# Fetching one chunk of edges in 68 with row DMAs of SyncE instead of a gather of GpSimd, in a four-layer graph network

## The chip, the cores and the metric

The kernel runs on one core of a Trainium2 chip. The metric is the device time of one execution in microseconds, from the first to the last instruction of the core with what lies around it; the time before is the median of three runs.

## The reference, cut to what matters

A graph of 12,500 nodes and 212,500 edges, sorted by destination, with 128 features per node. Four layers follow each other, each `x = x + layer(relu(layernorm(x)))`:

```
gat_conv twice:   e = leaky_relu(alpha_src[src] + alpha_dst[dst]); softmax of e over each dst
                  out = segment_sum(alpha[:, None] * h[src], dst)
transformer_conv: alpha = sum(q[dst] * k[src]) per head; softmax over each dst
                  agg = segment_sum(a * v[src], dst); then wo, layer norm, feed forward, layer norm
max layer:        msgs = z[dst] @ Wd + z[src] @ Ws + edge_weight * ww + bm
                  agg = segment_max(msgs, dst); then two dense layers
mean layer:       segment_sum(x[src], dst) / max(count, 1)
```

Each of the five aggregations (gat twice, transformer, max, mean) reads a row of a node table for every edge: `h[src]`, `k[src]` and `v[src]`, and so on.

## The kernel before

The kernel first prepares the edge lists: `prepared` (L406) brings the source numbers of the edges into the tile `IDX` (L463), in which column k holds the 128 source numbers of chunk k, one per partition. After that come five *edge passes*, `edge_pass` (L1298), one for each aggregation: gat1, gat2, attn, max and sum. Between them the dense work of a layer is done tile by tile at the end of each node tile (`after_gat1` and the like).

A pass walks over 98 node tiles of 128 nodes (T = 98). The 1,661 chunks of 128 edges are dealt out in *units* of 17 chunks (U = 17), a unit to a node tile, with a margin of three chunks to both sides. A unit's chunks form six groups (GS = 3), the last of them with two chunks. For every chunk `gather` (L1207) issues one indirect DMA from GpSimd's queue: 128 rows of the pass's table, picked by a column of `IDX`, into a slot of the tile `g` (L1212). The tables are rows of 66, 130, 264, 128 and 129 floats in the five passes, and `g` has 18, 18, 17, 20 and 24 buffers of one group each. `e1`, `chain` and `e2` work on the edges of a group; `batch` (L1240) multiplies one-hot matrices with the edge rows into `acc`; `ends` (L1271) loads `gt`, takes the result out of `acc`, merges it with `gt` (`listed_too`, L1280), and does the layer's dense work.

The order of the work is written out by hand. `edge_pass` puts each step as a Python generator at a *round*, with a rank; a unit is 24 rounds long (RU = 24), a group has 4. In every round the live generators advance by one step, the lowest rank first, and this fixes the order of instructions on each engine's queue. The gather of group i of unit u stands at round 24(u - 1) + 4i, its first use (`e1`) 24 rounds later. The loads of `se`, `st`, `x` and `gt`, and the stores of results (`o`, `xx`, `kv`, `u` and so on), all stand on SyncE's queue (SP), at their rounds, and SP issues them in this order: it waits at a store until the result is there, and what is behind it waits too. SP's DMAs use eight semaphores in turn, so that each DMA waits until the one eight before it has landed.

Of the kernel before, what the change touches and what calls it, by code (L numbers as in the profile page):

```python
# [65 lines left out]
def gnn_kernel(ctx, tc, a, out):  # L66
# [17 lines left out]
    ww_d = dram.tile([3, D], BF16, name="ww_d")  # L84
    feat_d = dram.tile([T, 5, EW], BF16, name="feat_d")
    last_d = dram.tile([T, 5, EW], BF16, name="last_d")
    ewf_d = dram.tile([3, CP * P], BF16, name="ewf_d")
    first_d = dram.tile([1, (CP + 16) * P], BF16, name="first_d")
    xd = dram.tile([NP, D], F32, name="xd")
# [198 lines left out]
    def chunks(out, x, on):  # L288

        o = out.rearrange("p (r b) -> p r b", b=RC)  # L290
        for b0 in range(0, RC, 4):
            n = min(4, RC - b0)
            px = psum([P, 4, P], "b", "px")
            for b in range(n):
                PE.transpose(px[:, b, :], x[:, (b0 + b) * P:(b0 + b + 1) * P], ident)
            yield
            on(o[:, :, b0:b0 + n].rearrange("p r b -> p b r"), px[:, :n, :])
# [108 lines left out]
    def prepared(wp):  # L406
        tn_i = wp.tile([P, 1], I32, name="tn_i")
        GP.iota(tn_i, pattern=[[0, 1]], base=0, channel_multiplier=P)
        tid = wp.tile([T, 1], I32, name="tid")
        GP.iota(tid, pattern=[[0, 1]], base=0, channel_multiplier=1)  # L410
        tn = wp.tile([P, 1], F32, name="tn")
        V.tensor_copy(tn, tn_i)
        tn1 = wp.tile([P, 1], F32, name="tn1")
        V.tensor_scalar_mul(tn1, tn, -1.0)
        tn2 = wp.tile([P, 1], F32, name="tn2")
        V.tensor_scalar_add(tn2, tn, float(P))
        yield

        w = rd_[:, 1:EW + 1]
        eq = wp.tile([T, EW - P], BF16, name="eq")
        long_ = wp.tile([T, 1], F32, name="long_")
        V.scalar_tensor_tensor(eq, w[:, P:], 0.0, w[:, :EW - P], op0=ALU.add, op1=ALU.is_equal,
                               accum_out=long_)
        yield
        f = wp.tile([T, 2], F32, name="f")
        V.tensor_scalar(f[:, 0:1], rd_[:, 0:1], tn[:T, :], long_, op0=ALU.is_ge, op1=ALU.max)
        V.tensor_scalar(f[:, 1:2], rd_[:, EW + 1:], tn2[:T, :], f[:, 0:1], op0=ALU.is_lt,  # L430
                        op1=ALU.max)
        V.tensor_scalar_min(f[:, 1:2], f[:, 1:2], 1.0)
        yield
        p2 = psum([P, P], "mm", "p2")
        PE.transpose(p2[:1, :T], f[:, 1:2], ident[:T, :T])
        yield
        flag = wp.tile([1, T], F32, name="flag")
        V.tensor_copy(flag, p2[:1, :T])
        zr = wp.tile([1, T], F32, name="zr")
        V.memset(zr, 0.0)  # L440
        ord_ = wp.tile([1, T], F32, name="ord_")
        V.tensor_tensor_scan(ord_, flag, zr, 0.0, op0=ALU.add, op1=ALU.add)
        V.tensor_copy(NOV, ord_[:, T - 1:T])

        at = wp.tile([1, T], F32, name="at")
        V.scalar_tensor_tensor(at, flag, -float(2 * T), ord_, op0=ALU.mult, op1=ALU.add)
        V.tensor_scalar_add(at, at, float(2 * T - 1))
        yield
        pfl = psum([P, P], "mm", "pfl")
        PE.matmul(pfl[:, :T], ones[0:1, :], flag, start=True, stop=True)  # L450
        p3 = psum([P, P], "mm", "p3")
        PE.transpose(p3[:T, 0:1], at, ident[0:1, 0:1])
        yield
        V.tensor_copy(FLAG, pfl[:, :T])
        at_i = wp.tile([T, 1], I32, name="at_i")
        V.tensor_copy(at_i, p3[:T, 0:1])
        GP.indirect_dma_start(out=list_d, in_=tid, in_offset=None,
                              out_offset=bass.IndirectOffsetOnAxis(ap=at_i[:, 0:1], axis=0),
                              bounds_check=T - 1, oob_is_err=False)
        SY.dma_start(LIST, list_d.rearrange("(p t) c -> p (t c)", p=1))  # L460
        yield

        yield from chunks(IDX, sd, V.tensor_copy)  # L463

        ch = wp.tile([P, RC * P], F32, name="ch")
        V.tensor_tensor(ch, dd[:, 1:], dd[:, :RC * P], ALU.not_equal)
        yield
        yield from chunks(FIRST, ch, S.copy)
        m = wp.tile([P, RC * P], BF16, name="m")
        S.mul(m, ch, -BIG)  # L470
        SY.dma_start(first_d[0, P:(CP + 1) * P].rearrange("(p f) -> p f", p=P), m)
        yield
        dl = w
        V.tensor_scalar(dl, w, tn1[:T, :], FAR, op0=ALU.add, op1=ALU.min)
        V.tensor_scalar_max(dl, dl, -1.0)
        yield
        xb = wp.tile([T, EW], BF16, name="xb")
        S.copy(xb, dl)
        SY.dma_start(feat_d[:, 2, :], xb)
        hi, lo = yield from square(wp, dl, [T, EW], "q")  # L480
        for k, y in ((3, hi), (4, lo)):
            SY.dma_start(feat_d[:, k, :], y)
        yield
# [648 lines left out]
    def last_rows(pool):  # L1132
# [9 lines left out]
        for c0 in range(0, EW, n):  # L1142
# [30 lines left out]
                SY.dma_start(last_d[:, k, c0:c0 + n], y)  # L1173
            yield

    class Pass:


# [10 lines left out]

        made, whole = True, True  # L1190

        def __init__(self):
            self.rhs, self.gs, self.f, self.fa, self.x, self.n0 = {}, {}, {}, {}, {}, {}
            self.st, self.se, self.acc = {}, {}, {}

# [6 lines left out]
        def x_load(self, t):  # L1202
            if self.source is not None:
                self.x[t] = features(self.source, t, self.width)
            yield

        def gather(self, u, i):  # L1207
            c, n = groups_of(u)[i]
            g = self.pool.tile([P, GS, self.wid], self.dt, name="g", bufs=self.bufs)
            for j in range(n):  # L1210
                k = u * U + c + j
                GP.indirect_dma_start(  # L1212
                    out=g[:, j, :], out_offset=None, in_=self.table,
                    in_offset=bass.IndirectOffsetOnAxis(ap=IDX[:, k:k + 1], axis=0))
            self.gs[u, i] = g
            yield
# [81 lines left out]
    def edge_pass(name, table, wid, dt, wids, work_of, post, extra=()):  # L1298
        nonlocal ps_now
        w = work_of  # L1300
        with tc.tile_pool(name=name, bufs=2) as pool, \
                tc.tile_pool(name="ps_" + name, bufs=1, space=PSUM) as pp, tc.manual_schedule():
            ps_now, w.pool, w.table, w.wid, w.dt, w.wids = (pp, w.banks), pool, table, wid, dt, wids
            cal = {}

            def at(r, rank, g):
                cal.setdefault(r, []).append((rank, g))

            for u in range(T):
                r0 = u * RU  # L1310
                at(r0 - RU, 0, w.load(u))
                at(r0 + RU - 4 - w.tail[0] * (u == T - 1), 0, w.load2(u))
                for i, _ in enumerate(groups_of(u)):
                    at(r0 - RU + i * RG, 0, w.gather(u, i))
                    at(r0 + i * RG, 5, w.e1(u, i))
                    if w.e2_at is not None:
                        e2_at = w.e2_at if u < T - 2 else w.e2_last or w.e2_at
                        at(r0 + e2_at[i] - w.tail[0] * (u == T - 1), 4, w.e2(u, i))
                if w.chain_at is not None:
                    at(r0 + w.chain_at - w.tail[0] * (u == T - 1), 3, w.chain(u))  # L1320
                n = len(w.batches(u))
                rt = r0 + w.tile_at
                loads = rt - RU
                rt -= w.tail[1] * (u == T - 2) + w.tail[2] * (u == T - 1)
                at(min(loads, rt + RU - 9 - 3 * (n - 1) - 2), 0, w.tile_load(u))
                at(rt, 0, w.x_load(u))
                for b in range(n):
                    at(rt + RU - 9 - 3 * (n - 1 - b), 2, w.batch(u, b, n))
                at(rt + RU - 4, 1, w.ends(u, post))
            for g in extra:  # L1330
                at(0, 1, g(pool))
            live, r = [], min(cal)
            while live or cal:
                live += cal.pop(r, [])
                live.sort(key=lambda g: g[0])
                live = [g for g in live if next(g[1], live) is not live]
                r += 1
# [116 lines left out]
        V.tensor_tensor(c, x, b, ALU.subtract)  # L1454

    class gat(Pass):
        chain_at, e2_at, tile_at = RU + 5, range(RU + 13, 2 * RU + 1, 2), 2 * RU

        def __init__(self, c, source=None):
# [116 lines left out]
            return r  # L1576

    class attn(Pass):
        bufs, source, width = 17, x2d, 2 * D
        chain_at, tile_at = RU + 7, 2 * RU + 2  # L1580
        e2_at = [RU + 15 + r for r in (0, 2, 4, 6, 7, 11)]
# [68 lines left out]
            return r  # L1650

    class maximum(Pass):
        feats, bufs, source, made = last_d, 20, xd, False
        tile_at, tail = 12, (0, 0, 8)
        banks = {"pm": 1, "x": 2, "acc": 1, "pg": 2, "mm": 2}
# [45 lines left out]
            return r  # L1701

    class total(maximum):
        bufs, made = 24, True
        tile_at, tail = 10, (0, 0, 0)
        banks = {"acc": 2, "mm": 2}
# [173 lines left out]
```

## Time and profile before

| what | value |
|---|---|
| median of three runs | 10,801.2 us (10,796.43 to 10,809.79) |
| profiled execution, its own time | 10,801.08 us |
| its span | 10,799.4 us |
| mean granted TensorE clock | 0.722 |
| gathers in the five passes (POOL, L1212) | 3,322 + 1,661 + 1,661 + 1,661 = 8,305 |
| first and last gather of gat1 | 161.1 us, 2,277 us |
| start of the gathers of gat2, attn, max, sum | 2,320.9, 4,442.4, 6,613.9, 8,713.8 us |
| DMA queue of POOL (q0) | 292,368 packets, 610.29 MB |
| DMA queue of SP (q1) | 463,932 packets, 519.87 MB |

The page gives busy time, share of the span and instructions of each engine first; then the costliest groups of instructions by line, with the count, the total and mean duration, and after the second bar the idle time of the engine just before them, with what ended most of it. "issue" means that the engine waited for nothing that the profile shows. Waits, branches and the issuing of plain DMAs are not counted as busy; they are seen in the timeline of the engine's queue, where SP is written SPq.

### The profile page before, as it was taken

How to read it: one execution, taken by the hardware profiler on the slowest of the kernel's cores; microseconds unless marked ns; L12 is line 12 of the kernel's file. 1: busy time of each engine (PE TensorE's matmuls, PEld its weight loads, DVE VectorE, ACT ScalarE, POOL GpSimd, SP SyncE). 2: the span in 40 equal slices, each digit the busy share in tenths (PEclk: the TensorE clock that was granted, in tenths of full speed). 3: DMA queues.
4: the chain of work that ended last, by engine and by line, in shares of the span. 5: the costliest groups of instructions: out<-in, count | busy, mean ns of one | idle time of the engine just before them, and what ended most of it. 6: DMA issues, size and time to landing. Idle time of an engine off the chain costs nothing. (4 is left out here: it accounts for less than half of the span.)

```text
span 10799.4 us, 149821 instructions
## 1 busy us (share of the span) xinstructions
PE 7520.8 (70%) x47184; PEld 5604.3 (52%) x47185; DVE 4569.7 (42%) x15187; ACT 4675.5 (43%) x13171; POOL 7916.2 (73%) x8330
## 2 busy tenths in 40 slices
PE   3676666656555556677777777888888866666666
PEld 2343333334444444566666666666666644444444
DVE  4555555544444444577777774333333310000000
ACT  4666666644444444355555554344434421111111
POOL 3777777767777777677777775777777767777777
PEclk6555555556677676799999998889888865555555
DMA  4222222224444444455555553333333323333333
GB/s 135 77 74 74 72 73 74 73 80 118 117 114 118 117 114 118 129 167 164 164 167 164 167 162 103 94 96 96 93 96 97 94 76 81 81 79 81 81 79 79
DMA packets 758382, 1143.66 MB, mean 106 GB/s; under 512 B 224040, under 2 KB 491511, under 8 KB 757471
## 3 DMA queue, kind: packets, MB, share of 16 engines
q0 software_dynamic: 292368, 610.29, 22.7%
q1 hardware_dynamic: 463932, 519.87, 14.9%
q8 instruction: 374, 6.13, 0.2%
q10 hardware_dynamic: 1268, 3.77, 0.1%
q14 instruction: 440, 3.60, 0.1%
HBM read 964.76 MB, written 168.43 MB: 105 GB/s over the span
## 5 line engine op out<-in xcount | busy, mean ns | idle before, releaser
L1212 POOL DMA_INDIRECT g<-t,IDX x3322 | 3156.3, 950 | 1173.2 <-issue 693.2
L1267 PE MATMUL acc<-xf,sef 128*128 128x131 f32 (+2 forms) x13458 | 2285.9, 320 | 563.3 <-ACT sef L1258 536.4
L1267 PEld LDWEIGHTS acc<-xf,sef 128*128 128x128 f32 x13458 | 1980.0, 222 | 736.1 <-ACT sef L1258 599.9
L1212 POOL DMA_INDIRECT g<-tkv,IDX x1661 | 1607.2, 968 | 547.5 <-issue 407.6
L1212 POOL DMA_INDIRECT g<-ts__83,IDX x1661 | 1568.6, 944 | 564.6 <-issue 359.1
L1212 POOL DMA_INDIRECT g<-th,IDX x1661 | 1572.3, 947 | 531.2 <-issue 409.0
L1267 PE MATMUL acc<-g,sef 128*128 128x129 f32 x4486 | 1360.2, 444 | 726.5 <-DMA g<-th,IDX 615.1
L1267 PEld LDWEIGHTS acc<-g,sef 128*128 128x128 f32 x4486 | 995.8, 302 | 1090.9 <-DMA g<-th,IDX 742.4
L1258 ACT CAST sef<-se 128x512 f32<-128x512 fp8e4 (+1 forms) x1755 | 1028.5, 598 | 438.1 <-PE acc L1267 432.5
L1282 DVE COPY_PREDICATED r<-FLAG,gt 128x129 f32<-128x129 int32 (+2 forms) x490 | 146.7, 299 | 2140.0 <-ACT r L1288 2076.6
L1683 DVE TENSOR_TENSOR_SCAN fm<-n,fm,pg 128x384 f32<-128x384 bf16 (+1 forms) x585 | 566.6, 969 | 935.0 <-PE pg L1680 933.7
L1495 PE MATMUL ex<-ADX,st 128*128 128x6 bf16 x4486 | 354.1, 174 | 835.2 <-ACT st L1109 372.2
L1495 PEld LDWEIGHTS <-st 128*128 128x128 fp8e4 x4486 | 328.7, 113 | 1005.3 <-ACT st L1109 565.3
L1500 ACT COPY lg<-g 128x3 f32<-128x3 f32 (+1 forms) x1172 | 226.6, 193 | 1142.0 <-DMA g<-t,IDX 1074.4
L1288 ACT COPY r<-acc 128x129 f32<-128x129 f32 (+2 forms) x392 | 105.9, 270 | 1308.0 <-PE acc L1267 1308.0
L1693 ACT COPY xf<-pt_f 128x384 f32<-128x384 f32 x586 | 270.6, 462 | 867.5 <-PE pt_f L1689 850.0
L1267 PE MATMUL acc<-xs,se 128*128 128x201 bf16 x2243 | 483.7, 368 | 229.6 <-ACT x L1553 118.1
L1124 PE MATMUL pm_se<-NF,fa 5*128 5x128 bf16 x4486 | 586.2, 266 | 0.0
L1418 DVE TENSOR_TENSOR_SCAN fw<-n,lt 17x384 f32<-17x384 bf16 (+1 forms) x294 | 303.2, 1031 | 545.4 <-PE lt L1430 545.4
L1109 ACT ACTIVATE st<-pm_st,ones 128x384 fp8e4<-128x384 f32 (+2 forms) x877 | 471.3, 537 | 121.1 <-PE pm_st L1116 121.1
L1613 PE MATMUL qe<-q,st 128*128 128x128 bf16 x6729 | 482.9, 222 | 23.8 <-DVE g L1618 16.7
L1689 PE MATMUL pt_f<-ident,fm 128*128 128x128 f32 x1661 | 342.5, 318 | 206.6 <-DVE xf L1692 141.4
(1098 smaller groups left out, 12350.4 us busy)
## 6 DMA issues: line engine op xcount, KB each, us to landing
se<-se_d SPq DMA_DIRECT2D x294, 368.0 KB
st<-st_d SPq DMA_DIRECT2D x196, 368.0 KB
g<-t,IDX POOLq DMA_INDIRECT x3322
n<-first_d SPq DMA_DIRECT2D x97, 544.0 KB
st_d<-st SPq DMA_DIRECT2D x98, 368.0 KB
se_d<-se SPq DMA_DIRECT2D x98, 368.0 KB
g<-tkv,IDX POOLq DMA_INDIRECT x1661
g<-ts__83,IDX POOLq DMA_INDIRECT x1661
```

The lines of the kernel that those rows point to most:

```text
L1109: S.activation(out, pm[:, :out.shape[1], :], AF.Relu, scale=-1.0, bias=ones[:, 0:1], saturate=False)
L1124: PE.matmul(pm[:, j, :], f[:, (c + j) * P:(c + j + 1) * P], NF, start=True, stop=True)
L1212: GP.indirect_dma_start(out=g[:, j, :], out_offset=None, in_=self.table, in_offset=bass.IndirectOffsetOnAxis(ap=IDX[:, k:k + 1], axis=0))
L1258: S.copy(se, self.se[t][:, at, :])
L1267: PE.matmul(acc[:, :m], se[:, j, :], x[:, i, :], start=(b == 0 and j == 0), stop=(b == n - 1 and j == len(ws) - 1))
L1418: V.tensor_tensor_scan(fw[:, s0 * P:(s0 + n) * P], n0[:, s0 * P:(s0 + n) * P], lt[:r, :n, :].rearrange("p j e -> p (j e)"), fw[:, s0 * P - ...
L1495: PE.matmul(ex[:, 6 * k:6 * k + 6], st, ADX[:, t, :, :].rearrange("p s v -> p (s v)"), start=(first and c0 == 0), stop=(stop and c0 + n - ...
L1500: S.copy(lg[:, 0, 1 + c0:1 + c0 + n, :], self.gs[u, i][:, :n, c + 1:c + 2])
L1613: PE.matmul(qe[0][:, k - c0, :], st, self.q[t][:, s * D:(s + 1) * D], start=(first and s == 0), stop=(stop and s == 2))
L1683: V.tensor_tensor_scan(fm[:, :m, :].rearrange("p j e -> p (j e)"), self.n0[u][:, cols], pg, self.prev, op0=ALU.add, op1=ALU.max)
L1689: PE.transpose(pt[:, j, :], fm[:, j, :], ident)
L1693: S.copy(ft[:, :m, :D], pt[:, :m, :])
```

## The change

In units 3, 7, 11 up to 95 of each pass (every fourth, 24 in all) the last of the 17 chunks isn't gathered by GpSimd any more. `fetch_rows` fetches it on SP's queue, row by row. It starts at round 24u - 80: it takes a tile `gx` with two slots (two buffers), loads the 128 source numbers of the chunk into one partition (`rw`), waits four rounds, and then issues 128 DMAs of one row each, spread evenly over 88 rounds, one or two to a round, ahead of everything else in the round (rank -1). For the addresses SP reads 16 numbers at a time from `rw` into registers. The last row is issued at about round 24u + 12, and the group's `e1` stands at 24u + 20. `gather` then uses `gx` in place of `g` for this group and issues one gather (chunk 16 of the unit, counted from one) into its first slot. The source numbers are stored once as integers in a new array `src_x`, in the preparation; for this the tile `ch` is written and read once ahead of its other use.

In the built program one row is two instructions on SP: a fused register operation (a copy and two multiplications, from the row's number to its address) and the DMA. A register load of 16 comes ahead of every sixteenth row. Over the five passes this makes 120 gathers fewer on POOL, and on SP 15,360 DMAs of a row, 15,360 fused register operations, 960 register loads and 120 loads of `rw` more. The other engines have the same work.

```diff
+    src_x = dram.tile([CP * P, 1], I32, name="src_x")
...
+        ch = wp.tile([P, RC * P], F32, name="ch")
+        V.tensor_copy(ch.bitcast(I32), sd)
+        SY.dma_start(flat(src_x), ch.bitcast(I32))
+        yield
         yield from chunks(IDX, sd, V.tensor_copy)
 
-        ch = wp.tile([P, RC * P], F32, name="ch")
         V.tensor_tensor(ch, dd[:, 1:], dd[:, :RC * P], ALU.not_equal)
...
+    RR = 16
+    row_regs = [SY.alloc_register(f"row{i}") for i in range(RR)]
...
+        by_row = None
+
         def __init__(self):
+            self.gx = {}
...
+        def row_units(self):
+            if self.by_row is None:
+                return [], 0
+            span = self.by_row * RU - 4
+            return [(u, RU // 2 - span) for u in range(T - 1) if u % self.by_row == self.by_row - 1
+                    and u * RU + RU // 2 - span >= -RU], span
+
+        def fetch_rows(self, u, span):
+            g = self.gx[u] = self.pool.tile([P, 2, self.wid], self.dt, name="gx", bufs=2)
+            rw = self.pool.tile([1, P], I32, name="rw", bufs=2)
+            e0 = (u * U + U - 1) * P
+            SY.dma_start(rw, src_x[e0:e0 + P, :].rearrange("(o f) c -> o (f c)", o=1))
+            for r in range(4):
+                yield
+            q = 0
+            for r in range(span - 4):
+                while q < P and q * (span - 4) < (r + 1) * P:
+                    if q % RR == 0:
+                        SY.load(row_regs, rw[0:1, q:q + RR])
+                    v = SY.snap(row_regs[q % RR], min_val=0, max_val=NP - 1)
+                    SY.dma_start(g[q:q + 1, 1, :], self.table[ds(v, 1), :])
+                    q += 1
+                yield
+
         def gather(self, u, i):
             c, n = groups_of(u)[i]
-            g = self.pool.tile([P, GS, self.wid], self.dt, name="g", bufs=self.bufs)
+            by_row = i == NG - 1 and u in self.gx
+            if by_row:
+                g, n = self.gx.pop(u), n - 1
+            else:
+                g = self.pool.tile([P, GS, self.wid], self.dt, name="g", bufs=self.bufs)
             for j in range(n):
...
+            units, span = w.row_units()
+            for u, r in units:
+                at(u * RU + r, -1, w.fetch_rows(u, span))
...
     class gat(Pass):
+        by_row = 4
```

`by_row = 4` is set in the same way in the classes of the attn, max and sum passes.

More of the change, by code (lines that the diff above doesn't have):

```diff
@@ L1578, in gnn_kernel @@
     class attn(Pass):
+        by_row = 4
         bufs, source, width = 17, x2d, 2 * D
@@ L1652, in gnn_kernel @@
     class maximum(Pass):
+        by_row = 4
         feats, bufs, source, made = last_d, 20, xd, False
@@ L1703, in gnn_kernel @@
     class total(maximum):
+        by_row = 4
         bufs, made = 24, True
```

## The prediction

> **What bounds the kernel now.** I read the page first: the busy shares and the costliest groups.
>
> ```profile
> PE 7520.8 (70%) x47184; PEld 5604.3 (52%) x47185; DVE 4569.7 (42%) x15187; ACT 4675.5 (43%) x13171; POOL 7916.2 (73%) x8330
> ...
> L1212 POOL DMA_INDIRECT g<-tkv,IDX x1661 | 1607.2, 968 | 547.5 <-issue 407.6
> ```
>
> 73% for POOL doesn't look like a bound. But in its group the idle time before the gathers is put down to "issue", a wait for nothing that the profile shows. So the second view is POOL's timeline, here 4 us of the sum pass.
>
> ```profile
> 9000.29 0.94 POOL L1212 DMA_INDIRECT g<-th,IDX  x1 [0.30 <-issue]
> 9001.54 0.94 POOL L1212 DMA_INDIRECT g<-th,IDX  x1 [0.30 <-PE acc L1267]
> 9002.79 0.94 POOL L1212 DMA_INDIRECT g<-th,IDX  x1 [0.30 <-issue]
> 9004.04 0.94 POOL L1212 DMA_INDIRECT g<-th,IDX  x1 [0.30 <-issue]
> ```
>
> A gather starts every 1.25 us: 0.94 busy and a fixed 0.30, the same where another engine is named as releaser. POOL never pauses. The third view asks whether that holds in all passes: the gathers inside a stretch of each pass (gat1, gat2, attn, max, sum), whose columns are the stretch, its length, POOL's busy time and the count.
>
> ```profile
> 600.00:2200.00 1600.00, 1210.65 (x1276) 0.50 0.29 73
> 2500.00:4300.00 1800.00, 1362.06 (x1438) 0.70 0.41 116
> 4600.00:6400.00 1800.00, 1368.63 (x1417) 0.98 0.57 165
> 6800.00:8600.00 1800.00, 1360.75 (x1442) 0.89 0.33 96
> 8900.00:10700.00 1800.00, 1361.73 (x1439) 0.57 0.31 80
> ```
>
> Length by count: 1.254, 1.252, 1.270, 1.248 and 1.251 us per gather, whatever the clock (0.50 to 0.98) and the row width. So each of the five passes is bound by POOL's rate of issuing gathers; a unit of 17 chunks takes 21.3, 21.3, 21.6, 21.2 and 21.3 us. The other engines wait for POOL: in the table of waits ACT, PE and its weight loads wait for the landing of g.
>
> The fourth view is the engine that gets the new work, SP. One unit of gat2:
>
> ```profile
> 3501.25 0.32 SPq L801 DMA_DIRECT2D tkv<-kv  x1
> 3504.65 0.34 SPq L808 DMA_DIRECT2D tq<-q__38865  x1
> 3505.04 0.28 SPq L1382 DMA_DIRECT2D n<-first_d  x1
> 3505.37 0.33 SPq L1274 DMA_DIRECT2D gt<-gen_d  x1
> 3515.43 0.32 SPq L786 DMA_DIRECT2D x2d<-xx  x1
> 3515.79 0.43 SPq L712 DMA_DIRECT2D x<-in_x  x1
> 3516.32 0.39 SPq L1229 DMA_DIRECT2D se<-se_d  x1
> 3516.81 0.38 SPq L1223 DMA_DIRECT2D st<-st_d  x1
> 3517.24 0.42 SPq L1563 DMA_DIRECT2D hs__39021<-t  x1
> ```
>
> A plain DMA takes SP 0.28 to 0.43 us, and the next begins about 50 ns later. These nine are 3.21 us, with gaps 3.65. The same sum over a unit of the others: gat1 3.20 in ten (3.7 with gaps), attn 3.44 in eight (3.8), max 3.12 in nine (3.6), sum 1.58 in four (1.8). SP is free for some 17.5 us of each unit (19.5 in sum), and I ask whether the rows fit.
>
> **What is removed.** 24 units in each of five passes lose one gather: 120 gathers x 1.25 us = 150 us. All lie on the path, so this is the whole possible gain (1.4%). A unit then has 16.75 gathers on average, and POOL's floor is 16.75 x 1.25 = 20.9 us.
>
> **What is added to SP.** For each of the 120 chunks: one load of 128 indices, 8 register loads of 16 each, 128 fused register operations (three each) and 128 DMAs of one row. Both ends of a row's cost are in the trace, on SP itself, before the first pass and with one register:
>
> ```profile
> L943 SPq TENSOR_LOAD <-NOV x4: 271/274/521, 162.8 to 170.1; - x4
> L943 SPq FUSED_REGOPS  x4: 147/147/159, 163.4 to 170.4; - x4
> ...
> L588 SPq DMA_DIRECT2D wwr<-in_L_gnn_Wm x1: 292/292/292, 35.2 to 35.2; - x1
> ```
>
> *A row.* A fused register operation is 0.147 us (three operations as here; these were comparisons, the new ones hold two multiplications). Loads of one 512-byte row took 0.339, 0.291 and 0.248 us (brow, L568) and 0.292 (wwr); I take 0.28. With two gaps of 0.05 less rounding: 0.147 + 0.28 + 0.09 = 0.52 us. No DMA with a register for its address ran before; below 0.248 + 0.147 + 0.09 = 0.485 it can't well go, since the address only adds work; above, 0.34 for the DMA gives 0.58.
> [...]
>
> *A register load of 16.* One register takes 0.27 us. If sixteen come in one read, it stays 0.27; that is the lower end. [...]
>
> *SP's time per unit* is then (128 x 0.52 + 8 x (load + 0.05) + 0.35 for the index DMA) / 4, plus what it did before. With 3.27: (66.6 + 26.6 + 0.35) / 4 = 23.4 us. In all: 27.1, 27.0, 27.2, 27.0 and 25.2 us per unit in the five passes, against 20.9 of POOL. SP becomes the bound.
>
> **How that reaches the path.** SP issues in order. Behind the rows stand the unit's other DMAs: gt, which DVE reads for r (L1282) a round or two after it is issued, the loads of se, st and x, and the stores of each pass. At 27 us of work for 21 us of pace SP falls behind until DVE waits for gt and PE for se and for the rows of gx; DVE and PE then free the buffers of g late, and POOL (17 to 24 of them) stops for them. Everything runs at SP's pace. SP's present waits for results (1900 us for o alone) vanish first; they are slack, not cost.
>
> **What costs nothing or little.** The rows' transfers: page part 3 has 463,932 packets of SP's queue in 14.9% of 16 engines' span, 55 ns each; 128 rows are 7 us of a DMA engine's time in 85 us, on one engine 8% where the busiest pass stands at 57%. If the cover went, the rows would land later, and they have 8 rounds (about 7 us) before their reader. A DMA of SP waits for the one eight before it: 8 x 0.52 = 4.2 us, and the longest wait of SP for a DMA in this trace is 4.2 us, in the preparation. 0 to 0.5 us per unit; I take 0. In the preparation: one DVE cast of 128x1664 (0.99 us at L352), one DMA of 832 KB, and the comparison L466 now waits until that DMA has read ch: 0 to 6 us, I take 2.
>
> **The sum.** The profiled execution took 10,801.1 us, span 10,799.4; the median of the runs is 10,801.2, so no correction. Rows are under way for about 96 of 98 units. Per unit: 27.1 - 21.3, 27.0 - 21.3, 27.2 - 21.6, 27.0 - 21.2, 25.2 - 21.3 = 5.8 + 5.7 + 5.6 + 5.8 + 3.9 = 26.8 us; x 96 = 2,573. 10,801 + 2,573 + 2 = **13,376 us**, 24% slower. With 0.16 to 0.24 us per register instead of 0.2 the loads are 2.7 to 3.9 us, 1.2 us per unit either way: 12,800 to 14,000 is this case's own range.
>
> **Rivals.** *SP fits (faster).* One mechanism: a register load of 16 costs what one costs, 0.27 us. Then SP needs (66.6 + 2.6 + 0.35) / 4 = 17.4 us per unit plus its old work: 21.1, 21.0, 21.2, 21.0, 19.2. POOL's floor is 20.9 (21.3 in attn). Gains: 0.2 + 0.3 + 0.3 + 0.2 + 0.4 = 1.4 us, x 96 = 134: 10,667 us. It decides at (21.3 - 3.65) x 4 / 128 = 0.55 us per row, loads shared out: with 0.52 per row a load must stay below about 0.4 us. For it: SP's 17.5 free us. Against it: SP would have to be busy all the time, while it still waits in order for o, xx, kv and u; any such wait that isn't covered is lost. *Loads partly overlapped*, four registers at a time: 0.27 + 3 x 0.25 = 1.0 us, (66.6 + 8.4 + 0.35) / 4 = 18.8; units of 22.5, 22.4, 22.6, 22.4 and 20.9: +4.2 us x 96 = 403: 11,200 us. *The register DMA is dearer*: every 0.1 us more per row is 3.2 us per unit, 1,540 us in all; with the long loads 14,900. *It doesn't do what it says*: excluded by the built program, which has 120 gathers fewer on POOL and 15,360 row DMAs more on SP.
>
> **Chances.** The long loads 0.45 (12,800 to 14,000). Loads partly overlapped or a dearer row with short loads 0.28 (10,830 to 12,800). Dearer rows with long loads 0.10 (above 14,000). SP just at POOL's pace, within 0.2% 0.05. SP fits 0.12. (0.2% is about what a measurement of this kernel tells from no change.) Faster 0.12, same 0.05, slower 0.83. The range, 10,780 to 14,300, leaves out SP fits and most of the dearest case, 0.2 together.
>
> **What would show it.** SP's TENSOR_LOAD at the new row loads: about 3.3 us (0.27 in the fast rival, 1.0 in the second). FUSED_REGOPS near 0.15, the row's DMA near 0.28. A gather count of 8,185, starting on average every 1.6 us instead of 1.25, with POOL's idle time put down to PE, DVE or ACT instead of issue. DVE r L1282 waiting for gt, which it hardly does now (25.9 us in 18 times), and SP's waits for o near zero. If SP still waits for o by many us per unit, SP isn't the bound and this prediction is wrong.

## The result and the profile after

The changed kernel takes 11,921.24 us (11,908.48 to 11,929.13, four runs) against 10,799.36 us for the kernel before (four runs): ratio 1.1039, 95% interval 1.1025 to 1.1053. It is slower, as forecast, but by 10.4% and not by 24%. The profiled execution took 11,925.77 us, its span is 11,924.1 us, 1,124.7 us more than before.

First the page, with POOL's busy time and the gathers of attn, and then the gathers inside a stretch of each pass (the stretch, its length, POOL's busy time, the count, and after it the granted TensorE clock).

```profile
PE 7705.8 (65%) x47184; PEld 5800.4 (49%) x47185; DVE 4574.8 (38%) x15188; ACT 4621.6 (39%) x13171; POOL 7791.1 (65%) x8210
...
L1254 POOL DMA_INDIRECT g<-tkv,IDX x1613 | 1554.3, 964 | 923.9 <-DVE xf L1689 422.3
```

```profile
500.00:2300.00 1800.00, 1283.64 (x1353) 0.50 0.27 70
2600.00:4600.00 2000.00, 1361.29 (x1438) 0.69 0.37 106
4950.00:7050.00 2100.00, 1338.76 (x1390) 0.90 0.48 141
7450.00:9650.00 2200.00, 1372.68 (x1455) 0.79 0.27 79
10000.00:11800.00 1800.00, 1361.42 (x1439) 0.57 0.31 82
```

Length by count is now 1.33, 1.39, 1.51 and 1.51 us per gather in gat1, gat2, attn and max, and still 1.25 in sum. In the first four passes POOL waits for other engines (in attn for DVE's xf, which frees the buffers of g), and is no longer the bound. In sum it still is. From the first and last gather of each pass the 1,125 us are made up like this:

| where | us more |
|---|---|
| gat1, gat2, attn, max (first to last gather) | 103, 185, 332, 378 |
| sum | -30 |
| between the passes (43.7, 41.9, 58.7, 25.4 us before; 71.9, 63.6, 79.0, 97.2 after) | 142 |
| ahead of the first gather (161.1 to 175.7 us) | 15 |

The sum pass gained the 30 us that 24 gathers of 1.25 us are worth. The other four lost 998.

Now SP's new instructions, by their lines: in each, minimum, median and maximum in ns, then the first and last start.

```profile
L1239 SPq TENSOR_LOAD <-rw x960: 991/1231/1898, 178.4 to 11858.4; - x192
...
L1240 SPq FUSED_REGOPS  x15360: 44/44/60, 179.4 to 11869.6; - x200
...
L1241 SPq MOVE gx<-ts__84 x3072: 29/29/38, 7324.4 to 9800.2; - x192
L1241 SPq DMA_DIRECT2D gx<-ts__84 x3072: 224/228/389, 7324.4 to 9800.3; - x192
```

A row is three instructions, not two (a register move comes with the DMA), and yet shorter than I had put it: from one row's DMA to the next is 419 ns in the median. A load of 16 registers takes 1.23 us in the median and 1.26 in the mean. By these, a unit costs SP (128 x 0.419 + 8 x (1.26 + 0.05) + 0.35) / 4 = 16.1 us on top of its old 3.7. That is 19.8 us, less than POOL's floor of 20.9. So SP has the time, and the prediction's own rule would now say "SP fits". It doesn't fit. The waits say where to look; the columns are the time in all, how often, and the longest. First those of SP at its stores in the kernel before, and all that DVE waited for gt there (time and how often):

```profile
SPq L919 <- DVE o L917: 1900.2, 98, 27.0
SPq L864 <- DVE st L688: 1554.4, 98, 19.1
SPq L902 <- DVE st L688: 1464.6, 98, 18.9
SPq L786 <- DVE st L688: 882.6, 97, 35.0
```

```profile
  DMA gt<-gen_d: 25.9, 18
```

And in the changed kernel, DVE first, then SP:

```profile
DVE r L1324 <- ACT r L1330: 1842.1, 97, 21.6
DVE r L1324 <- DMA gt<-gen_d: 1553.8, 381, 35.4
```

```profile
SPq L907 <- DVE st L693: 601.9, 98, 15.0
SPq L869 <- DVE st L693: 527.7, 98, 16.3
SPq L791 <- DVE st L693: 291.6, 97, 6.5
SPq L924 <- DVE o L922: 252.8, 98, 19.2
```

DVE now waits for gt in 381 tiles, and SP still waits at a store once in every tile of the passes max (L907, xd), attn (L869, xd), gat2 (L791, x2d) and sum (L924, out). Before, almost only SP waited; now DVE waits for SP, and SP for DVE. The timeline of SP's queue shows it in one unit of max (start, length, what; several of a kind are put together): first before, then after, and the third fence has DVE's merge with gt in it.

```profile
7508.54 0.32 SPq L902 DMA_DIRECT2D xd<-x  x1
...
7512.10 0.43 SPq L1274 DMA_DIRECT2D gt<-gen_d  x1
```

```profile
9490.41 0.71 SPq L1241 DMA_DIRECT2D gx<-ts__84  x2
9500.36 0.35 SPq L907 DMA_DIRECT2D xd<-x  x1
9500.91 2.32 SPq L1241 DMA_DIRECT2D gx<-ts__84  x6
...
9504.66 0.37 SPq L913 DMA_DIRECT2D th<-h  x1
9505.22 6.02 SPq L1241 DMA_DIRECT2D gx<-ts__84  x11
9511.30 0.36 SPq L1316 DMA_DIRECT2D gt<-gen_d  x1
```

```profile
9513.38 0.31 DVE L1324 COPY_PREDICATED r<-FLAG,gt 128x129 f32<-128x129 int32 x1 [5.17 <-DMA gt<-gen_d]
```

SP stands idle from 9491.1 to 9500.36 at the store of x, then issues 17 rows, four loads and a store for 11 us, and only then gt, for which DVE had been waiting 5.17 us. With gt DVE makes the next tile's x, whose store SP then waits for. It is a ring: store, gt, merge, dense work, store. Mean times around it, taken from the start times of tiles 20 to 80 of each pass, in us:

| pass | period before | store to next gt | gt to merge | merge to store | period after | store to next gt | gt to merge | merge to store |
|---|---|---|---|---|---|---|---|---|
| gat1 | 21.23 | 12.46 | 3.70 | 5.07 | 22.32 | 14.79 | 2.07 | 5.47 |
| gat2 | 21.30 | 12.15 | 6.88 | 2.27 | 23.62 | 19.12 | 2.22 | 2.27 |
| attn | 21.63 | 1.16 | 3.41 | 17.06 | 25.50 | 5.07 | 2.27 | 18.16 |
| max | 21.27 | 3.52 | 6.02 | 11.74 | 25.98 | 10.96 | 1.95 | 13.07 |
| sum | 21.27 | 1.34 | 18.82 | 1.12 | 20.98 | 15.81 | 4.03 | 1.12 |

In the changed kernel gt has landed 1.8 to 2.1 us after its issue (medians of these tiles in the five passes; 2.4 to 3.5 before), so two us from gt to its merge are the transfer; what was above that before I take for slack. It was 1.7 us in gat1, 4.9 in gat2, 1.4 in attn, 4.0 in max and 16.8 in sum. The rows put 2.3, 7.0, 3.9, 7.4 and 14.5 us more between store and gt. Where that is clearly more than the slack, in gat2, attn and max, the ring sets the period. In gat1 the two are close (2.3 against 1.7), and SP waits for the pass's table rows (L755) only 80.2 us in 68 tiles, so there the ring is the least clear.

In attn and max the way from merge to store has grown too, by 1.1 and 1.3 us. The granted clock of TensorE, whose matmuls lie on this way, fell there: from first to last gather from 0.96 to 0.89 in attn and from 0.89 to 0.79 in max. Two runs without the gathers, told below, bear on it: i2, with rows and ring, has a clock of 0.85 and 0.79 there, and i3, with the rows but not this ring, 0.96 and 0.89 again, with a way of 17.2 and 11.2 us. So this part comes with the ring and not with the rows; how much of it is the clock wasn't separated.

### The profile page after: what moved, and what is told of

The parts are those of the page before. It is cut to its first block, busy times and chain, and to the rows that moved or that the text cites. A ratio compares the mean times of both kernels' runs of the same rounds, so it can differ in the third digit from the quotient of the medians.

```text
span 11924.1 us, 197664 instructions
## 1 busy us (share of the span) xinstructions
PE 7705.8 (65%) x47184; PEld 5800.4 (49%) x47185; DVE 4574.8 (38%) x15188; ACT 4621.6 (39%) x13171; POOL 7791.1 (65%) x8210
## 5 line engine op out<-in xcount | busy, mean ns | idle before, releaser
L1254 POOL DMA_INDIRECT g<-t,IDX x3226 | 3058.8, 948 | 1534.0 <-issue 810.5
L1309 PE MATMUL acc<-xf,sef 128*128 128x131 f32 (+2 forms) x13458 | 2379.9, 330 | 509.7 <-ACT sef L1300 484.7
L1309 PEld LDWEIGHTS acc<-xf,sef 128*128 128x128 f32 x13458 | 2079.2, 232 | 677.1 <-ACT sef L1300 538.9
L1254 POOL DMA_INDIRECT g<-ts__84,IDX x1613 | 1521.9, 944 | 979.9 <-issue 396.9
L1254 POOL DMA_INDIRECT g<-tkv,IDX x1613 | 1554.3, 964 | 923.9 <-DVE xf L1689 422.3
L1254 POOL DMA_INDIRECT g<-th,IDX x1613 | 1526.3, 946 | 588.7 <-issue 376.6
L1309 PE MATMUL acc<-g,sef 128*128 128x129 f32 x4294 | 1299.0, 442 | 701.4 <-DMA g<-th,IDX 593.3
L1309 PEld LDWEIGHTS acc<-g,sef 128*128 128x128 f32 x4294 | 953.1, 301 | 1045.0 <-DMA g<-th,IDX 704.6
L1660 PE MATMUL qe<-q,st 128*128 128x128 bf16 x6729 | 520.5, 232 | 21.4 <-DVE g L1665 13.6
L1737 PEld LDWEIGHTS pt_f<-ident,fm 128*128 128x128 f32 x1661 | 222.6, 169 | 634.8 <-DVE xf L1740 536.5
```

The source lines that it names most:

```text
L1254: GP.indirect_dma_start(out=g[:, j, :], out_offset=None, in_=self.table, in_offset=bass.IndirectOffsetOnAxis(ap=IDX[:, k:k + 1], axis=0))
L1309: PE.matmul(acc[:, :m], se[:, j, :], x[:, i, :], start=(b == 0 and j == 0), stop=(b == n - 1 and j == len(ws) - 1))
L1660: PE.matmul(qe[0][:, k - c0, :], st, self.q[t][:, s * D:(s + 1) * D], start=(first and s == 0), stop=(stop and s == 2))
L1737: PE.transpose(pt[:, j, :], fm[:, j, :], ident)
```

## The experiments

*Theories.* Order (A): SP has the time for the rows, but they stand between a store and gt on a queue that runs in order, and the ring costs the time. Capacity (B): SP has too much to issue, whatever the order. A third (C): a chunk by rows costs its reader something fixed, however full SP is.

**First, a limit of these runs.** On each of the seven chips that ran the experiments the unedited kernel before took about 14,950 to 15,070 us, not 10,799. In its near twin e4 the gathers still start 1.25 us apart where they follow each other (8 of them from 14,003.26 to 14,011.99 us), but engines start late after the work recorded ahead of them: in the sum pass, at 14,011.99 us, ACT's copy of acc starts 4.1 us after the end of TensorE's last recorded matmul (0.04 us at 10,208.64 in the profile of before). A row's DMA can then last 1,399 ns, as the changed kernel's own second run (g1) shows beside the L1241 lines above, which had 224 ns as minimum and 389 as maximum:

```profile
L1241 SPq DMA_DIRECT2D gx<-ts__84 x3072: 2/228/1399, 10766.2 to 13599.6; - x192
```

In the traces of such runs many waits end for which no instruction is found that ended them ("remote" in the views; in e4 DVE's g at L1618 waited so for 1,299.2 us, 181 times); among the 200 costliest groups of waits of before, after, i2, i3, i4 and i6 there is none. What causes this, no run here shows. I call such runs stretched. They carry something that the result doesn't have, so I rest the verdict on the last six runs, where it was gone, and report what the stretched ones say against it.

**e1 and f1: gt a unit earlier** (twice, on two chips). The load moves from `ends` into `tile_load`:

```diff
         def tile_load(self, t):
+            gt = self.gts[t] = self.pool.tile([P, XW], F32, name="gt", bufs=4)
+            SY.dma_start(gt[:, :self.wids], gen_d[rows(t), :self.wids])
...
         def ends(self, t, post):
-            gt = self.pool.tile([P, XW], F32, name="gt")
-            SY.dma_start(gt[:, :self.wids], gen_d[rows(t), :self.wids])
-            self.gt = gt
+            self.gt = self.gts.pop(t)
```

> The changed kernel, with the load of gt issued a unit earlier, together with the load of se, so that it no longer stands just ahead of its reader behind the rows. Theory A (order): in the changed kernel SP is busy 18 to 21 us of a unit, and the rest of the 23 to 25 us is lost in a loop: gt is issued late behind rows, DVE waits for it (2.0, 6.1, 2.7 and 5.0 us per unit in gat1, gat2, attn and max), the stores that depend on it come late, and SP waits for them. Without the loop every pass falls to POOL's floor of 16.75 gathers: 10,660 to 10,750 us, DVE's wait for gt near zero. Theory B (capacity): SP simply has too much to issue; the time stays at 11,900, within 50.

> The changed kernel with the gt load moved into tile_load, a whole unit ahead of its reader, so that rows no longer stand in front of it on SP's queue; SP issues the same instructions. Order theory (A: SP has the time, gt behind the rows is what comes late, and the rest is a loop that starts there): the 1,550 us that DVE waited for gt go, gathers fall back to 20.9 to 21.3 us per unit, total 10,660 to 10,750 us. Capacity theory (B: SP has too much to issue): DVE's wait moves to another SP load or to the stores, total 11,850 to 11,950 us. In between, gt is one of several in-order waits of SP's queue.

17,381.54 and 17,399.65 us, ratios 1.1621 (1.1602 to 1.1641) and 1.1623 (1.1605 to 1.1640) to the kernel before on the same chip. Neither theory's number came, because the scale was another. DVE's wait for gt is gone, and the time is longer than that of the changed kernel (g1 below).

**e2: registers loaded once per chunk** (`if q == 0:` for `if q % RR == 0:`; the rows repeat the first 16 source numbers).

> The changed kernel with one register load of 16 per fetched chunk instead of eight, so that the 128 rows repeat the first 16 source numbers (those edges get wrong rows; the same bytes and the same number of DMAs). It takes 7 x 1.28 / 4 = 2.2 us of SP's time from each unit. Theories A and B: gat1 and gat2 fall to the floor of 20.9 us, attn and max from 25.0 to 22.8: 96 x (1.7 + 2.2 + 2.2 + 2.2) = 800 us less, 11,120. Theory C (the rows land late at their reader, and SP's issue time doesn't matter): no change, 11,900.

16,592.57 us, ratio 1.1097 (1.1078 to 1.1115). That is 327 us under g1 below, on another chip: less time on SP does shorten the kernel, by less than the 800 us expected.

**e3 and f2: rows in one unit of eight** (`by_row = 8`).

> The changed kernel with by_row = 8: one chunk in every eighth unit, 12 per pass, spread over twice as many rounds. Theories A and B: SP needs 11.6 us per unit and keeps ahead of DVE; POOL's floor with 60 gathers fewer is 10,801 - 75 = 10,726. Theory C (each chunk fetched by rows costs its own delay): half of the loss of 1,122 us remains, 11,340.

> The rows in one unit of eight (twice the rounds, so half the row rate; half as many gathers removed, 60 x 1.25 us = 75 us). Theories A and B both: SP is no longer short, total 10,730 us, under the kernel before. Theory C (each chunk by rows costs what it costs, whatever the rate; then half the loss): 11,360 us.

15,388.4 and 15,406.83 us, ratios 1.0286 (1.0269 to 1.0303) and 1.0292 (1.0276 to 1.0308). Set against g1 below, half the rows cost less than a quarter as much: in these runs the cost isn't one per row.

**e4: gt early in the kernel before**, without rows.

> The kernel before, with only the earlier load of gt. All theories: no change, 10,800 within 0.2%, because DVE waits for gt only 26 us in all there and POOL sets the pace.

14,966.11 us, ratio 1.0003 (0.9996 to 1.0009). By itself the earlier gt is worth nothing and costs nothing, in a stretched run.

**f3: rows in the sum pass only** (`by_row = None` in the other three classes).

> Rows in the sum pass only; the other four passes as in the kernel before. In the changed kernel the sum pass kept a gather every 1.25 us and its units took 20.9 us against 21.3 before. Theories A and B: 96 x 0.31 = 30 us less than before, about 10,770 us (ratio 0.997). If the gain of that pass was only work shifted across its edge, ratio 1.000 or above.

15,797.67 us, ratio 1.0553 (1.0539 to 1.0567): a loss of 830 us in the very pass that gained 30 us in the profile of after. So these runs have a bound that the first ones didn't have.

**f4: gt early and stores later**, each store two or more yields behind its data:

```diff
-        SY.dma_start(xd[rows(t), :], x)
         yield
         yield from norm(x, RS[:, t:t + 1], NM[:, t:t + 1])
+        SY.dma_start(xd[rows(t), :], x)
```

> As f1, and every store of a tile's results (t2, x2d, tkv, tq, xd, ts, th, out) is issued two or more yields later than its data is computed, so that SP does not stand waiting for it. SP's instructions are the same. Order theory: SP's waits for stores (2,000 us in the changed kernel) go, gathers every 1.25 us, 10,660 to 10,720 us; if f1 is there already, the stores add nothing. Capacity theory: no gain over the changed kernel, 11,850 to 11,950 us.

17,346.48 us, ratio 1.1595 (1.1577 to 1.1613).

**g1: the changed kernel, unedited.**

> The changed kernel itself, unedited, beside the kernel before on the same chip, as the reference for the first two sets of runs, in which the kernel before took 14,967 us instead of 10,799 us. If the slower chip stretches both alike, the ratio is 1.10 and the time 16,500 us there. Order theory: gt early (1.162) and stores late (1.160) should have been under this kernel's ratio; if the ratio of this one is 1.16 as well, neither moved anything there, which speaks for the capacity theory or for another limit on those chips.

16,919.63 us, ratio 1.1310 (1.1273 to 1.1347). DVE waited 5,319.5 us for gt here. In e1, f1 and f4 that wait is gone, and they are still 427 to 480 us slower than g1. From first to last gather of each pass, e1's units are longer than g1's in gat1 and gat2 (38.3 against 35.1, 36.8 against 33.6 us) and shorter in max (27.5 against 29.0). As it stands this speaks against order in the first two passes. Why, stays open.

**h1 to h3: less of TensorE's work** (before, changed, and changed with gt early):

```diff
-            for j, w in enumerate(ws):
+            for j, w in enumerate(ws[:1]):
...
-                for s in range(3):
-                    PE.matmul(qe[0][:, k - c0, :], st, self.q[t][:, s * D:(s + 1) * D],
+                PE.matmul(qe[0][:, k - c0, :], st, self.q[t][:, :D], start=first, stop=stop)
```

> The kernel before with work left out of TensorE: of each batch of up to four chunks only the first chunk's product into acc is made, and in attn one of the three products into qe. POOL, SP, DVE and ACT keep every instruction. In the runs so far the kernel before took 14,967 us, and TensorE's signals came up to 24 us after its last recorded matmul, while instructions of SP stood at multiples of 0.70 us just after bursts of matmuls. If those bursts are what stretches the runs here, this one falls back to about POOL's bound, 10,500 to 11,000 us; if not, it stays near 15,000 us.

> The changed kernel with the same work left out of TensorE. To be set against the run before it: order theory and capacity theory both want it longer by about the 1,120 us that the change cost, if TensorE's load has no part in it; if the change's cost needs TensorE's load, the two are equal to within 100 us.

> The changed kernel with gt loaded a unit earlier and the same work left out of TensorE. Order theory: within 100 us of the reduced kernel before, or under it. Capacity theory: as long as the reduced changed kernel.

14,295.57, 16,332.93 and 17,095.08 us: 0.950 (0.9472 to 0.9527), 1.0854 (1.0822 to 1.0885) and 1.1360 (1.1327 to 1.1393) of the kernel before. My idea that bursts of matmuls stretch these runs is not borne out: with fewer of them h1 is still far above 11,000 us. And h3, with gt early, is 762 us longer than h2, where order had asked for the time of h1 and capacity for that of h2; again the loss is in gat1 and gat2.

**i1 and i2: the gathers left out**, before and changed. POOL fills a group with one plain DMA of fixed rows:

```diff
-            for j in range(n):
-                k = u * U + c + j
-                GP.indirect_dma_start(
-                    out=g[:, j, :], out_offset=None, in_=self.table,
-                    in_offset=bass.IndirectOffsetOnAxis(ap=IDX[:, k:k + 1], axis=0))
+            GP.dma_start(g[:, :n, :], self.table[:n * P, :].rearrange("(j p) c -> p j c", p=P))
```

> The kernel before with its gathers left out: POOL fills each group of three chunks with one plain DMA of fixed rows of the table (6 DMAs per unit in place of 17 gathers), so that POOL bounds nothing. What is left then sets the time: TensorE, busy 7,500 us in the profile of before, so about 8,000 to 9,000 us if the runs here are not stretched once two thirds of the gathers' signals are gone; 12,000 us or more if they still are.

> The changed kernel with the gathers left out in the same way; SP still fetches its 128 rows in one unit of four. SP's own floor shows itself here, POOL's bound being gone. From the profile of after SP's instructions with the gaps between them fill 17.8 to 20.8 us of a unit, 97.1 us over the five passes. If that is its whole need (order theory: SP has the time, and only the order of its queue loses it), 96 x 97.1 us and some 400 us around them, 9,300 to 9,900 us. Capacity theory (the waits of SP's queue for stores belong to the need, whoever bounds the rest): units of 23 to 25 us as in the changed kernel, 11,500 to 11,900 us.

8,985.19 and 12,089.15 us, ratios 0.5966 (0.5948 to 0.5983) and 0.8026 (0.8001 to 0.8051). The stretching is gone: in i2 a row takes 419 ns from DMA to DMA, a register load 1.23 us, and a row's DMA 263 ns at the 95th percentile, all as in the profile of after. POOL no longer bounds anything, and yet i2 has nearly the time of the changed kernel. Its units, worked out from first to last group of a pass over 97, are 23.1, 23.4, 28.3, 25.3 and 18.4 us (the expectations below have 22.3 for gat1, and 20.2 for gat1 of i1, which leave out a stop at the pass's start; with it 23.1 and 20.9); those of the changed kernel 22.9, 23.3, 25.2, 25.3 and 21.1. So in gat1, gat2 and max POOL had next to no part in the period. The same waits stand out, DVE's first, SP's in the second fence:

```profile
DVE r L1320 <- DMA gt<-gen_d: 3487.5, 473, 19.2
```

```profile
SPq L869 <- DVE st L693: 691.5, 98, 18.3
SPq L907 <- DVE st L693: 598.2, 98, 15.0
```

The number is near the one that capacity had named (11,500 to 11,900 us) and far from order's 9,300 to 9,900. But it doesn't yet tell a full queue from a ring, since i2 keeps the ring, which my figure for order had left out. The next four do.

**i3 and i5: i2 with gt early, and with stores late as well.**

> The changed kernel with gathers left out (as i2, 12,089 us) and gt loaded a unit earlier. In i2 SP's units were 22.3, 23.4, 28.3, 25.4 and 18.4 us, of them 2.3, 3.5, 8.3, 6.2 and 1.1 us idle in waits for stores, whose data DVE makes after it waited for gt (3,490 us). Order theory (a ring of SP and DVE through gt): DVE's wait goes, SP's idle with it, units of SP's own 17 to 20 us, about 9,800 us. Capacity theory: the wait only moves to the next load or store on SP's queue, 11,700 to 12,100 us.

> As i3, with each store two or more yields later than its data. Order theory: about 9,800 us, and less than i3 if stores still stopped SP there. Capacity theory: as i2. If this one reaches 9,800 us and i3 does not, it is the wait for stores, not gt, that is the ring.

10,498.78 and 10,508.18 us, 0.7011 (0.6989 to 0.7033) and 0.7018 (0.6996 to 0.7039) of the kernel before. Moving one load per tile, with the same instructions on SP, takes away 1,590 us of the 3,104 us that the rows cost here (the kernel before differs by 0.6% between the two chips). SP's waits at the stores, in i3:

```profile
SPq L869 <- DVE st L693: 49.4, 6, 14.9
...
SPq L907 <- DVE st L693: 37.5, 4, 15.5
```

From 98 times each they fall to 6 and 4, with the stores where they were; later stores add nothing. The units become 21.7, 20.6, 21.8, 20.1 and 18.0 us, of which SP's instructions with their small gaps fill 20.7, 19.9, 20.1, 19.2 and 17.3. What is left over the kernel without rows (i1) is about 1,510 us, and there SP is nearly full: this is what capacity is worth here. But 1,030 us of it lie in the sum pass, which POOL bounds as long as there are gathers. In the first four passes the rows cost about 1,960 us, and the earlier gt takes some 1,540 of them away. The time lies between order's 9,800 us and capacity's 11,700, nearer to order's, which took the units for SP's fill alone and put too little around the passes.

**i4 and i6: i2 with one unit in eight, and the same with gt early.**

> Gathers left out, rows in one unit of eight. SP's own need falls to about 12 us per unit, and the rest of the kernel takes 20.2, 16.9, 22.4, 19.8 and 7.4 us per unit without rows (i1, 8,985 us). If only SP's fill matters: 9,000 to 9,700 us (the sum pass then at SP's 9 to 10 us). If a row costs its reader a fixed delay whatever SP's fill, half of what the rows cost in i2: 10,500 us.

> Gathers left out, rows in one unit of eight, gt loaded a unit earlier. In i4 (10,206 us, the same without gt early) SP was idle 8 to 13 us of each unit and DVE still waited 1,847 us for gt, so there SP's fill cannot be the reason. If the place of gt on the queue is (order theory), that wait goes, and the first four passes come to the times without rows (20.2, 16.9, 22.4, 19.8 us per unit in i1), 9,000 to 9,500 us in all. If rows cost their reader something of their own, 9,900 us or more.

10,206.48 and 9,225.46 us, 0.6816 (0.6795 to 0.6837) and 0.6131 (0.6113 to 0.6148). In i4 SP is idle for 8 to 13 us of a unit in the first four passes, so it is not full, and rows still cost 1,221 us over i1. DVE's wait for gt in i4, and then in i6:

```profile
DVE r L1320 <- DMA gt<-gen_d: 1846.6, 385, 12.9
```

```profile
DVE r L1320 <- DMA gt<-gen_d: 27.1, 3, 9.8
```

With gt out of the ring all but 240 us of the 1,221 are gone, as order had said (9,000 to 9,500 us), and attn falls from 25.2 to 21.0 us per unit. A fixed price per chunk (C) is near the time of i4 (10,500 us) but not that of i6, where it had asked for 9,900 or more. Here capacity has no part in the first four passes: 981 us hang on the place of gt (the kernel before differs by 0.5% between the two chips). Not all of it need be the rows' doing, as i1 too waits 582.4 us for gt, and i1 with gt early wasn't run.

## Why the prediction was right and wrong

The direction came true, the sum did not. Two terms of SP's work were too large, by 7.2 us per unit together, most of it the register load; and SP's waits, which the prediction put at nothing, cost 2.3 to 6.1 us per unit in the four passes that lost time. The steps one by one:

*POOL bounds all five passes before; the gain can be 150 us at most.* Right as far as it was tried: in sum, where nothing else came in the way, 24 gathers gave 30 us.

*A row, 0.52 us.* Too dear: 0.419. I took the fused operation from comparisons (0.147 us; it took 0.044) and the DMA from loads at the start (0.28; it took 0.228, plus 0.029 for a move). The bound of 0.485 from below was wrong, because I took rows of other work for the least that this work can cost. The error is 0.10 x 128 / 4 = 3.2 us per unit.

*A load of 16 registers, 3.27 us.* This is the largest mis-sized term. It puts 0.2 us on each register after the first, which no run shows: the load took 1.23 us in the median, which with 0.27 for one register leaves 0.064 for each further one. The error is 2.0 x 8 / 4 = 4.0 us per unit. The rival "loads partly overlapped", with 1.0 us, was near the load's price, though no run shows its steps of 0.25 us. With both terms right the sum would have been 19.8 us per unit and "SP fits", 10,667 us.

*"SP's present waits for results vanish first; they are slack, not cost."* This is the step that failed in kind, and its error went the other way. It holds only if the result doesn't depend on what SP still has to issue. Here it does. Per unit, in us:

| | gat1 | gat2 | attn | max | sum |
|---|---|---|---|---|---|
| predicted work of SP | 27.1 | 27.0 | 27.2 | 27.0 | 25.2 |
| SP's instructions and gaps under 0.12 us, measured | 20.6 | 19.9 | 20.1 | 19.1 | 17.8 |
| SP idle | 2.3 | 3.4 | 5.1 | 6.1 | 3.3 |
| unit | 22.9 | 23.3 | 25.2 | 25.3 | 21.1 |

In gat2, attn and max the unit is SP's work plus idle time, nearly all of it the wait for a store that waits for SP's own gt (2.9, 4.9 and 5.7 us). In gat1 the idle time is spread over the stores of three tiles (se, gr, st), and it wasn't shown that they hang on gt. The rival "SP fits" had named this, "any such wait that isn't covered is lost", without a price. The price is the row of idle time. That the two errors have different signs, so that the measured time lay inside the range, was luck. In sum, where POOL stayed the bound, the forecast of 3.9 us more per unit had the wrong sign.

*How that reaches the path*: gt late, DVE late, buffers of g late, POOL stops. The waits of the changed kernel show this chain; i3 and i6 take its first link away, and in the first four passes most of the loss goes with it, in runs without the gathers. That with the gathers the same edit would do the same wasn't shown: the runs that tried it were stretched, and became longer. *"If SP still waits for o by many us per unit, SP isn't the bound"*: it waits 252.8 us (2.6 per unit) in sum, where POOL is the bound. As a test of the other passes the sentence was wrong. SP can wait at stores and set the pace.

*The preparation, 2 us.* It is 15 us to the first gather. *The time between the passes* had no term in the sum; it grew by 142 us. When POOL has issued the last gather of one of the first four passes, DVE still has 4, 4, 4 and 5 tiles to merge (3, 3, 3 and 1 before), and the next pass's gathers start only after these tiles' rows are stored (the last store of th in max starts at 9,865.5 us, the first gather of sum at 9,868.8). One tile more in the first three gaps and four more in the last fit the 28, 22, 20 and 72 us: POOL, no longer the bound, ends a pass further ahead of its readers.

*Would an earlier gt make the change pay?* By i3's units, and POOL's 21.1 of the sum pass as the least, the five passes would take 21.7, 21.1, 21.8, 21.1 and 21.1 us against 21.8, 21.4, 21.8, 21.4 and 21.4 before: 1.0 us x 97, about 100 us less than before. That is an estimate, a bold one with SP filled to 92 to 97%, and the time between the passes, 142 us more in the changed kernel, could undo it. No version that beats the kernel before was measured.

## What to carry to other kernels

An engine's idle time on a queue that runs in order isn't room for new work if it waits there for something that hangs on what it issues later. Draw the ring first (store, load, use, store), and set its slack, here 1.4 to 17 us, against what is put between two of its steps. A load that doesn't depend on the tiles before it, like gt, can stand far ahead of its reader; in the runs without the gathers that took away most of what the ring cost.

## What the runs showed of the hardware

- On SP, a row DMA with its address in a register takes 228 ns, its move 29 and a fused register operation (a copy and two multiplications) 44, against 147 for one with comparisons; one row follows the other in 419 ns (medians of the changed kernel's profile). A load of 16 registers from SBUF takes 1.23 us (L1239), of one 0.27 (L943, before).
- The granted clock of TensorE fell from 0.96 to 0.89 in attn and from 0.89 to 0.79 in max, where its busy share fell from 75% to 70% and from 86% to 77% (first to last gather), and it was 0.96 and 0.89 again in i3, without the waits.
- The same program took 10,799 us in the runs of the result and about 14,950 to 15,070 on seven chips in the experiments. There a gather still lasts 946 to 948 ns in the mean (g1; 944 to 968 in the profile of before), and engines start late after the work recorded ahead of them (4.1 us in a tile of e4, against 0.04 before). It went away when the gathers were left out. Neither fewer matmuls (h1, 5% less) nor an earlier gt (e4) did that. Whether it is the chip or something else that differed between the two sets of runs isn't known.
